# Block products for the first gated step, block sums on GpSimd, and an order that favours open PSUM banks

## The chip, the cores and the metric

The kernel runs on one core of one Trainium2 chip. The metric is the device time of one execution in microseconds; the kernel before takes 1395.11 us (median of three runs, 1395.05 to 1396.01). The profile of one execution has a span of 1394.1 us from its first to its last instruction; the runs lie about 1 us above it.

## What is computed

The input is `x`, 64 samples of 256 nodes with 128 features, float32, and one 256 x 256 adjacency matrix `adj` that all samples share. Four graph layers follow one another, each in the frame `x = layernorm(x + layer(x))`: two attention layers, a gated layer of five steps, and a Chebyshev layer of order three. For this change the gated layer (layer 2) matters most:

```python
def step(h, _):
    m_in = jnp.einsum('nm,bmd->bnd', in_matrix, h)     # adj @ h, the "left product"
    m_out = jnp.einsum('nm,bmd->bnd', out_matrix, h)   # the same matrix here
    av = jnp.concatenate([m_in, m_out], axis=-1)
    u3 = h @ u3_w.T + u3_b
    z = jax.nn.sigmoid(av @ w3_w.T + w3_b + u3)
    r = jax.nn.sigmoid(av @ w4_w.T + w4_b + u3)
    hv = jnp.tanh(av @ w5_w.T + w5_b + (r * h @ u5_w.T + u5_b))
    h = (1.0 - z) * h + z * hv
```

Layer 3 needs one more left product, `adj @ x`.

## The kernel before

**Units and lanes.** The 64 samples are worked off in 32 units of two samples. Ten lanes of SBUF buffers hold ten units at a time; `spawn` lists all four layers of a unit as tasks, and when a unit is done its lane takes the next one. So up to ten units, each in another layer or step, share the engines.

**The order.** No engine order is written by hand. Every instruction is a `Task` with an engine, an assumed duration, what it reads and writes, and the PSUM banks that it uses. `Plan.run` plays these tasks through in advance with the assumed durations and latencies: whenever an engine is free it takes, of the tasks that are ready, the one with the smallest key, `first(t)`: the place of the unit in the queue times 43 us plus the task's due time in the unit. A task that opens a PSUM bank (`t.takes`) is ready only if one of the eight banks is free. The order so found is the order in which each engine's instructions stand; on the chip each engine works its own list from the front, and semaphores hold back an instruction whose inputs are not there.

**The left product, plain form.** `left` (L812 to L818) makes `adj @ h` for one sample by two matmuls of 128x256; a unit of two samples needs four. ScalarE then copies the bank into `m` (L886). A float32 matmul appears in the trace as two records, so the four are eight records of line L816.

**The left product, fast form.** `left_fast` (L820) treats the 256 x 256 matrix as 2 x 2 blocks of 128 and the unit's two samples as two columns of blocks, and does the 2 x 2 by 2 x 2 block product by seven block products rather than eight (Winograd's form of Strassen's method):

- Four block sums of the operand `h`, in three VectorE instructions, L826 (two blocks at once, 128x256), L828 and L829 (128x128 each), into the tile `four`, which lies on the lane's buffer `r`; the trace calls that buffer `e`. The sums of the matrix blocks are made once, at the start, on GpSimd (L476 to L480), in two layouts, `adjTf` for steps 1 to 4 and `adjf` for layer 3.
- Seven matmuls of 128x128 (L833) into two banks `x` and `y`; three read blocks of `h`, four read block sums.
- A ScalarE copy of one product (L845) and four VectorE additions (L860, L863, L865, L866) that merge the products into `m`.

`FAST = (1, 2, 3, 4, 5)` says where the fast form is used: steps 1 to 4 of layer 2, and 5 is layer 3's left product; step 0 uses the plain form. Units 0 and 1 and the last unit use the plain form in some steps (`far`).

**The rest of a step.** L890 makes five products of 128x512 into two banks: `gT[3]` with `h`, three of gate weights with `m`, and `u5T` with the reset state. ScalarE applies tanh three times (L901, L909, L918), VectorE combines (L904, L916, L920, L922), transposes in blocks (L930), and two hops of DMA through DRAM (L933, L936) bring the new state back in the layout that the next left product reads. Where a list of tasks is given as `after`, the product waits for them as well; `lefts[1:2]` in L895 lets the product with `h` follow the second left product of its own step.

**GpSimd** before makes the small steps of the layer norms (L584 to L595) and little else.

Of the kernel before, what the change touches and what calls it, by code (L numbers as in the profile page):

```python
# [16 lines left out]
STEPS = 5  # L17
LANES = 10
LEAD = 10
BANKS = 8  # L20
BL = 32
FAST = (1, 2, 3, 4, 5)
NORM = (0, 1, 2, 3)
SCALES = True
SMALL = ("ve", "cu", "d", "elu", "shift")
# [6 lines left out]
PERIOD = 43e3  # L32
TAIL = 0.3
LATE = 6
# [3 lines left out]
DIRECT_ROWS = 3  # L38
XDIRECT = 10
START = 35e3  # L40
R2 = 1
R3 = 1.5

# [23 lines left out]
class Plan:  # L67
# [17 lines left out]
    def add(self, eng, ns, fn, reads=(), writes=(), after=(), wait=0, group=None, dma=False):  # L85
        t = Task(eng, ns, fn, self.unit, wait, dma or eng == "sp")
        for c in reads:
            t.deps.update(c.writers)
            c.readers.append(t)
        for c in writes:  # L90
            if c.bank and not c.writers:
                t.takes.append(c)
            if group is None or c.group is not group:
                c.waits = {w for o in (c, *c.over) for w in (*o.writers, *o.readers)} - {t}
                c.writers, c.readers, c.group = [], [], group
            t.deps.update(c.waits)
            if c.bank and c.writers:

                t.deps.add(c.writers[0])
            c.writers.append(t)  # L100
        t.deps.update(after)
        t.deps.discard(t)
        for c in {id(c): c for c in (*reads, *writes) if c.bank}.values():
            c.users += 1
            t.banks.append(c)
        t.step = self.step = self.step + 1
        t.layer = self.layer
        t.rank = self.rank
        self.tasks.append(t)
        return t  # L110
# [90 lines left out]
def kernel(  # L201
# [28 lines left out]
    nc = tc.nc  # L230
# [3 lines left out]
    NU = B // UB  # L234
    T = UB * N
    G = UB * NC
    PE, DVE, ACT, POOL = "pe", "dve", "act", "pool"
# [12 lines left out]
    plan = Plan([psum.tile([P, 512], F32, tag=f"ps{k}", name=f"ps{k}") for k in range(BANKS)])  # L250
    add = plan.add
# [142 lines left out]
    def product(ps, at, n, lhs, lhs_ap, rhs, rhs_ap):  # L394
        add(PE, mm_ns(n), lambda: nc.tensor.matmul(ps.ap[:, at : at + n], lhs_ap(), rhs_ap(), start=True, stop=True,
                                                   skip_group_check=True), (lhs, rhs), (ps,))
# [50 lines left out]
    gT = transposed("gT", [(gs[0], gs[0].ap), (gs[1], gs[1].ap), (gs[2], gs[2].ap), (u3, u3.ap)])  # L447
# [35 lines left out]
    adjTf = fast_blocks("adjTf", adjTp)  # L483
    adjf = fast_blocks("adjf", adjT) if 0 in FAST or STEPS in FAST else None
# [21 lines left out]
    X = {}  # L506

    def gd(ap):
        return ap.rearrange("p (g d) -> p g d", g=G)
# [307 lines left out]
                ps.ap[:, b * N : (b + 1) * N], lhs(b, mc), mat.ap[:, mc, :],  # L817
                start=(mc == 0), stop=(mc == NC - 1)), (src, mat), (ps,))  # L818

    def left_fast(src, blk, mat, s, p1, m):  # L820


        four = gd(s.ap)
        ss = object()

        add(DVE, 360, lambda: nc.vector.tensor_sub(  # L826
            four[:, 0:2], blk(slice(2, 3)).to_broadcast([P, 2, D]), blk(slice(0, 4, 3))), (src,), (s,), group=ss)
        add(DVE, 220, lambda: nc.vector.tensor_sub(four[:, 2:3], four[:, 1:2], blk(slice(0, 1))), (src, s), (s,), group=ss)  # L828
        add(DVE, 220, lambda: nc.vector.tensor_add(four[:, 3:4], four[:, 2:3], blk(slice(1, 2))), (src, s), (s,), group=ss)  # L829
        x, y = bank(), bank()  # L830

        def one(ps, at, lhs, k, c, cells, after=()):
            add(PE, mm_ns(P) + 4, lambda: nc.tensor.matmul(  # L833
                ps.ap[:, at * P : (at + 1) * P], lhs(), mat.ap[:, k, c * P : (c + 1) * P], start=True, stop=True,
                skip_group_check=True), (*cells, mat), (ps,), after, group=four)

        def a(g):
            return lambda: blk(slice(g, g + 1))[:, 0]

        def sm(k):  # L840
            return lambda: four[:, k]


        one(x, 0, a(0), 0, 0, (src,))
        add(ACT, 280, lambda: nc.scalar.copy(p1.ap[:, 0:P], x.ap[:, 0:P]), (x,), (p1,))  # L845
        one(x, 1, a(1), 1, 0, (src,))
        one(y, 3, a(3), 3, 1, (src,), s.writers[-1:])
        one(y, 1, sm(0), 3, 0, (s,))
        one(y, 0, sm(1), 2, 0, (s,))
        one(x, 2, sm(2), 2, 1, (s,))  # L850
        one(y, 2, sm(3), 1, 1, (s,))
        mv = gd(m.ap)

        ms = object()

        def pv(ps):
            return gd(ps.ap)


        add(DVE, 400, lambda: nc.vector.tensor_tensor(  # L860
            mv[:, 0:4:3], pv(x)[:, 1:3], p1.ap[:, 0:P].rearrange("p (o n) -> p o n", o=1).to_broadcast([P, 2, P]), op=ALU.add),
            (x, p1), (m,))
        add(DVE, 400, lambda: nc.vector.tensor_tensor(  # L863
            mv[:, 1:3], pv(y)[:, 0:2], mv[:, 3:4].to_broadcast([P, 2, P]), op=ALU.add), (y, m), (m,))
        add(DVE, 240, lambda: nc.vector.tensor_add(mv[:, 3:4], pv(y)[:, 0:1], mv[:, 2:3]), (y, m), (m,))  # L865
        add(DVE, 400, lambda: nc.vector.tensor_add(mv[:, 1:3], pv(y)[:, 2:4], mv[:, 1:3]), (y, m), (m,))  # L866

    def layer2(u, L):
        h, ht = turned(u, L, -1), X[u]
        for step in range(STEPS):  # L870
            m, at = L["m"], len(plan.tasks)
            fast = step in FAST and far(u, step - 1)
            ps_m = None if fast else bank()
            if fast and not step:
                left_fast(ht, lambda g: ht.ap.rearrange("p b c d -> p (b c) d")[:, g], adjf, L["r"], L["z"], m)
            elif fast:
                left_fast(ht, lambda g: gd(ht.ap)[:, g], adjTf, L["r"], L["z"], m)
            for b in range(0 if fast else UB):
                if ht is X[u]:
                    left(ps_m, ht, b)  # L880
# [8 lines left out]
            def product(ps, w, c, rhs, start, stop, after=()):  # L889
                add(PE, mm_ns(T), lambda: nc.tensor.matmul(ps.ap, w(), rhs.ap, start=start, stop=stop,  # L890
                                                           skip_group_check=True), (c, rhs), (ps,), after)


            lefts = [t for t in plan.tasks[at:] if t.eng == PE]
            product(ps_g, lambda: gT.ap[:, 3], gT, h, True, False, lefts[1:2])  # L895
            product(ps_g, lambda: gT.ap[:, 1], gT, m, False, True)
            r, z, v = L["r"], L["z"], L["v"]

# [14 lines left out]
            if not step:  # L913
                add(ACT, 600, lambda h=h, new=new, part=part: nc.scalar.mul(new.ap, h.ap, part), (h,), (new,))
                h = new
# [54 lines left out]
    def layer3(u, L):  # L970
        xT = turned(u, L, STEPS)
        aT, s = L["m"], L["z"]
        if STEPS in FAST and far(u, STEPS):
            left_fast(X[u], lambda g: X[u].ap.rearrange("p b c d -> p (b c) d")[:, g], adjf, L["r"], L["z"], aT)
            tail = [t for t in plan.tasks[-4:-3]]
        else:
            ps_a = bank()
            for b in range(UB):
                left(ps_a, X[u], b)
            add(ACT, 500, lambda: nc.scalar.copy(aT.ap, ps_a.ap), (ps_a,), (aT,))  # L980
            tail = list(ps_a.writers)

        ps = [bank() for _ in range(NC)]

        def view(c):
            return ps[c].ap.rearrange("p (k b d) -> p k b d", k=2, b=UB)

        for k, src in enumerate((xT, aT)):
            for c in range(NC):
                for b in range(UB):  # L990
                    add(PE, mm_ns(N), lambda k=k, src=src, c=c, b=b: nc.tensor.matmul(  # L991
                        view(c)[:, :, b, :], bn(src.ap)[:, b, c * P : (c + 1) * P], w3.ap[:, k],
                        start=(k == 0 and b == 0), stop=(k == 1), skip_group_check=True), (src, w3), (ps[c],), tail)
        for c in range(NC):
            add(ACT, 300, lambda c=c: nc.scalar.copy(s.ap[:, c * N : (c + 1) * N], ps[c].ap[:, N : 2 * N]), (ps[c],), (s,), group=ps)
        for c in range(NC):
            for mc in range(NC):
                add(PE, mm_ns(N), lambda c=c, mc=mc: nc.tensor.matmul(  # L998
                    ps[c].ap[:, 0:N], a2T.ap[:, mc, c * P : (c + 1) * P], s.ap[:, mc * N : (mc + 1) * N],
                    start=False, stop=(mc == NC - 1), skip_group_check=True), (a2T, s), (ps[c],))  # L1000
        pairs = [(ps[c], lambda c=c: view(c)[:, 0]) for c in range(NC)]
        if u >= NU - 2:
            layernorm_last(u, pairs)
            return
        layernorm(u, L, pairs, swap=True)
        add("sp", 450, lambda: nc.sync.dma_start(out_u[u], X[u].ap), (X[u],), ())
# [10 lines left out]
    def first(t):  # L1017
        if t.rank is not None:
            return t.rank * PERIOD
        if t.unit < 0:  # L1020
            return t.due - 1e6
        return (t.unit if t.unit < NU - LANES else NU - 1 - LATE - (NU - 1 - t.unit) * TAIL) * PERIOD + t.due

    with tc.manual_schedule():
        for t in plan.run(spawn, range(NU), first):
# [31 lines left out]
```

The softmax here doesn't subtract the row's maximum and nothing guards it: scores larger than these inputs give would overflow.

## Time and profile before

| what | value |
|---|---|
| time, median of 3 | 1395.11 us |
| span in the profile | 1394.1 us |
| L890, matmul 128x512, all forms, chain share | 49% |
| L833, matmul 128x128, chain share | 17% |
| L816, matmul 128x256, chain share | 5% |
| L886, ScalarE copy of a plain left product | 39 times, 585 ns each |
| L860, L863, L865, L866, the merge of a fast one | 152 times each; 417, 418, 281, 413 ns |
| L845, ScalarE copy in the fast form | 152 times, 267 ns |

The chain share says how much of the span lies on the chain of work that ended last, by line. Mean durations are those of one instruction on its engine. The busy time of a matmul record is modelled, and records overlap, so a matmul's cost on TensorE is read from the distance between the starts of successive records and not from its mean duration.

### The profile page before, as it was taken

Reading aid. Unit: us, or ns where it says so; the run is one execution under the profiler, and the core shown is the slowest. Engines: PE = TensorE matmul, PEld = TensorE weight load, DVE = VectorE, ACT = ScalarE, POOL = GpSimd, SP = SyncE. Lnnn points to the kernel's source line nnn. Section 1 sums busy time; section 2 is a strip of 40 time slices with the busy share of each in tenths; the row PEclk is TensorE's granted clock in tenths of the full one; section 3 lists DMA queues with packets and bytes.
Section 4 is the critical chain, followed back from the end, with each engine's and each line's share of the span. In section 5 each row is a group of like instructions: output and inputs, shape, how many; then the busy total and the mean of one; then the engine's idle time right before and its main releaser. Section 6 shows DMA issues by size and latency. Waiting matters only on the chain.

```text
span 1394.1 us, 21842 instructions
## 1 busy us (share of the span) xinstructions
PE 1385.5 (99%) x6537; PEld 963.8 (69%) x6537; DVE 1191.1 (85%) x2849; ACT 911.2 (65%) x2094; POOL 257.9 (18%) x488
## 2 busy tenths in 40 slices
PE   9999999999999999999999999999999999999998
PEld 8776576776666766676676667676666666667776
DVE  6788898999988888888898899889888888999763
ACT  6887636556765767666676778787755555565454
POOL 3111020112112112122121122132111110112212
PEclk9999999999999999999999999999999999999999
DMA  4134554455455454554455555554463543544521
GB/s 126 32 62 99 114 120 86 117 108 131 109 114 112 98 130 95 122 127 102 108 108 111 128 110 110 118 114 103 108 129 94 119 105 86 115 114 106 129 52 47
DMA packets 530068, 147.03 MB, mean 105 GB/s; under 512 B 456480, under 2 KB 495136, under 8 KB 529952
## 3 DMA queue, kind: packets, MB, share of 16 engines
q1 hardware_dynamic: 529152, 145.13, 46.6%
q8 instruction: 52, 0.85, 0.3%
q14 instruction: 64, 0.52, 0.2%
q10 hardware_dynamic: 800, 0.52, 0.1%
HBM read 81.10 MB, written 64.46 MB: 104 GB/s over the span
## 4 chain that ended last, share of the span: by engine, by line
PE 98%; ACT 1%; DVE 1%; DMA 0%; issue 0%; SPq 0%; POOL 0%; POOLq 0%; DVEq 0%; ACTq 0%
PE ps L890 49%; PE ps L833 17%; PE ps L991 8%; PE ps L816 5%; PE ps L738 4%; PE ps L998 4%; PE ps L775 4%; PE ps L787 2%; PE ps L733 2%; PE ps L662 2%; ACT p L711 0%; DMA u<-rowu 0%; PE ps L348 0%; PE ps L955 0%; PE ps L528 0%; PE ps L571 0%
## 5 line engine op out<-in xcount | busy, mean ns | idle before, releaser
L890 PE MATMUL ps<-m,gT 128*128 128x512 f32 x960 | 464.1, 593 | 0.0
L890 PEld LDWEIGHTS ps<-m,gT 128*128 128x128 f32 x960 | 170.8, 190 | 124.9 <-issue 107.8
L909 ACT ACTIVATE e<-ps,bias 128x512 f32<-128x512 f32 x160 | 109.7, 687 | 159.0 <-PE ps L890 156.5
L901 ACT ACTIVATE e<-ps,bias 128x512 f32<-128x512 f32 x160 | 109.9, 687 | 98.9 <-PE ps L890 97.0
L833 PEld LDWEIGHTS ps<-adjTf,ht 128*128 128x128 f32 x726 | 117.6, 191 | 74.3 <-issue 60.1
L584 POOL TENSOR_SCALAR ve<-st 128x4 f32<-128x4 f32 x110 | 36.3, 330 | 690.5 <-DVE st L582 662.3
L890 PE MATMUL ps<-e,u5T 128*128 128x512 f32 x320 | 162.4, 592 | 0.0
L587 POOL TENSOR_TENSOR rstd<-ve,nhalf 128x4 f32<-128x4 f32 x126 | 142.0, 1127 | 66.5 <-DVE ve L584 59.5
L833 PEld LDWEIGHTS ps<-adjTf,e 128*128 128x128 f32 x968 | 127.4, 192 | 19.2 <-issue 17.7
L833 PE MATMUL ps<-adjTf,e 128*128 128x128 f32 x968 | 139.6, 275 | 0.0
L918 ACT ACTIVATE p<-ps,bias 128x512 f32<-128x512 f32 x160 | 110.2, 689 | 40.5 <-PE ps L890 38.4
L833 PE MATMUL ps<-adjTf,ht 128*128 128x128 f32 x726 | 123.7, 275 | 0.3 <-DVE m L860 0.3
L920 DVE SCALAR_TENSOR_TENSOR p<-e,p 128x512 f32<-128x512 f32 x160 | 109.4, 685 | 16.5 <-ACT p L918 16.0
L890 PEld LDWEIGHTS ps<-e,u5T 128*128 128x128 f32 x320 | 59.3, 190 | 61.4 <-issue 51.6
L890 PE MATMUL ps<-xT,gT 128*128 128x512 f32 x192 | 97.5, 594 | 0.4 <-ACT xT L530 0.4
L860 DVE TENSOR_TENSOR m<-ps,e 128x256 f32<-128x256 f32 x152 | 63.0, 417 | 25.1 <-PE ps L833 21.2
L764 ACT ACTIVATE e<-m,esd 128x256 f32<-128x256 f32 x116 | 82.2, 766 | 0.0
L904 DVE SCALAR_TENSOR_TENSOR e<-e,xT 128x512 f32<-128x512 f32 x96 | 65.7, 684 | 15.5 <-ACT e L901 13.5
L863 DVE TENSOR_TENSOR m<-ps,m 128x256 f32<-128x256 f32 x152 | 63.3, 418 | 16.0 <-PE ps L833 14.1
L541 DVE STREAM_TRANSPOSE p<-x 128x512 f32<-128x512 f32 x61 | 67.3, 1104 | 11.1 <-ACT x L606 11.0
L738 PEld LDWEIGHTS ps<-ht,p 128*128 128x128 f32 x512 | 65.9, 190 | 12.9 <-issue 12.0
L738 PE MATMUL ps<-ht,p 128*128 128x130 f32 x512 | 68.5, 274 | 0.0
(191 smaller groups left out, 2784.0 us busy)
## 6 DMA issues: line engine op xcount, KB each, us to landing
hb<-p SPq DMA_DIRECT2D x182, 256.0 KB, 2.3
ht<-hb SPq DMA_DIRECT2D x484, 64.0 KB, 2.6
xT<-hb SPq DMA_DIRECT2D x244, 64.0 KB, 2.5
m<-row SPq DMA_DIRECT2D x58, 256.0 KB, 3.8
hb<-p SPq DMA_DIRECT2D x124, 64.0 KB, 1.8
ht<-hb SPq DMA_DIRECT2D x31, 256.0 KB, 3.0
out_dram<-x SPq DMA_DIRECT2D x30, 256.0 KB, 2.4
m<-in_x_dram SPq DMA_DIRECT2D x88, 64.0 KB, 2.3
```

Source lines behind the costliest of these rows:

```text
L541: add(DVE, 1050, lambda: nc.vector.transpose(v.ap.rearrange("p (a g i) -> p g a i", g=G, i=BL), X[u].ap.rearrange("p b c (j a) -> p (b c) ...
L587: add(POOL, 1050, lambda: nc.gpsimd.tensor_tensor(rstd.ap, ve.ap, nhalf.ap, op=ALU.pow), (ve, nhalf), (rstd,))
L738: add(PE, mm_ns(D + 2), lambda b=b, ic=ic, kc=kc, yv=yv: nc.tensor.matmul(yv()[:, ic, :], p.ap[:, b * NC + kc, ic * P : (ic + 1) * P], h.a ...
L764: add(ACT, 600, lambda g=g, b=b: nc.scalar.activation(e.ap[:, g, :].rearrange("p (c n) -> p c n", c=NC), ev()[:, b], AF.Prelu, bias=esd.ap ...
L816: add(PE, mm_ns(N), lambda b=b, mc=mc: nc.tensor.matmul(ps.ap[:, b * N : (b + 1) * N], lhs(b, mc), mat.ap[:, mc, :], start=(mc == 0), stop ...
L833: add(PE, mm_ns(P) + 4, lambda: nc.tensor.matmul(ps.ap[:, at * P : (at + 1) * P], lhs(), mat.ap[:, k, c * P : (c + 1) * P], start=True, st ...
L890: add(PE, mm_ns(T), lambda: nc.tensor.matmul(ps.ap, w(), rhs.ap, start=start, stop=stop, skip_group_check=True), (c, rhs), (ps,), after)
L901: add(ACT, 600, lambda ps_g=ps_g, up=up: nc.scalar.activation(r.ap, ps_g.ap, AF.Tanh, bias=bias2.ap[:, 1:2], scale=0.5 / up), (ps_g, bias2 ...
L909: add(ACT, 600, lambda ps_g=ps_g, up=up: nc.scalar.activation(z.ap, ps_g.ap, AF.Tanh, bias=bias2.ap[:, 0:1], scale=0.5 / up), (ps_g, bias2 ...
L918: add(ACT, 600, lambda ps_v=ps_v, up=up: nc.scalar.activation(v.ap, ps_v.ap, AF.Tanh, bias=bias2.ap[:, 2:3], scale=1 / up), (ps_v, bias2), ...
L920: add(DVE, 600, lambda: nc.vector.scalar_tensor_tensor(v.ap, z.ap, 1.0, v.ap, op0=ALU.add, op1=ALU.mult), (v, z), (v,))
L991: add(PE, mm_ns(N), lambda k=k, src=src, c=c, b=b: nc.tensor.matmul(view(c)[:, :, b, :], bn(src.ap)[:, b, c * P : (c + 1) * P], w3.ap[:, k ...
```

## The change

It does four things. Step 0 joins `FAST`, so the gated layer's first left product is made by seven block products too. `BY_POOL` moves the three block-sum instructions from VectorE to GpSimd, in all six places, with durations of their own for the planner. In fast steps, the product with `h` now follows the third merging addition and not the second block product, so that its bank is opened later. And `HASTE` takes 20 us off the planner's key for a TensorE, ScalarE or VectorE task that works on a PSUM bank that is already open, so that banks are emptied and closed sooner. (`ht=ht` in the lambdas only binds the tile at that time.)

```diff
-FAST = (1, 2, 3, 4, 5)
+FAST = (0, 1, 2, 3, 4, 5)
+BY_POOL = (0, 1, 2, 3, 4, 5)
...
+HASTE = {"pe": 20e3, "act": 20e3, "dve": 20e3}
...
-    def left_fast(src, blk, mat, s, p1, m):
+    def block_sums(src, blk, s, by_pool):
         four = gd(s.ap)
         ss = object()
-        add(DVE, 360, lambda: nc.vector.tensor_sub(
+        by, eng = (POOL, nc.gpsimd) if by_pool else (DVE, nc.vector)
+        wide, narrow = (830, 480) if by_pool else (360, 220)
+        add(by, wide, lambda: eng.tensor_sub(
             four[:, 0:2], blk(slice(2, 3)).to_broadcast([P, 2, D]), blk(slice(0, 4, 3))), (src,), (s,), group=ss)
-        add(DVE, 220, lambda: nc.vector.tensor_sub(four[:, 2:3], four[:, 1:2], blk(slice(0, 1))), (src, s), (s,), group=ss)
-        add(DVE, 220, lambda: nc.vector.tensor_add(four[:, 3:4], four[:, 2:3], blk(slice(1, 2))), (src, s), (s,), group=ss)
+        add(by, narrow, lambda: eng.tensor_sub(four[:, 2:3], four[:, 1:2], blk(slice(0, 1))), (src, s), (s,), group=ss)
+        add(by, narrow, lambda: eng.tensor_add(four[:, 3:4], four[:, 2:3], blk(slice(1, 2))), (src, s), (s,), group=ss)
+        return four
+
+    def left_fast(src, blk, mat, s, p1, m, by_pool):
+        four = block_sums(src, blk, s, by_pool)
...
             lefts = [t for t in plan.tasks[at:] if t.eng == PE]
-            product(ps_g, lambda: gT.ap[:, 3], gT, h, True, False, lefts[1:2])
+            merge = plan.tasks[at:][-4:]
+            product(ps_g, lambda: gT.ap[:, 3], gT, h, True, False, merge[2:3] if fast else lefts[1:2])
...
-        return (t.unit if t.unit < NU - LANES else NU - 1 - LATE - (NU - 1 - t.unit) * TAIL) * PERIOD + t.due
+        soon = HASTE.get(t.eng, 0) if t.banks and not t.takes else 0
+        return (t.unit if t.unit < NU - LANES else NU - 1 - LATE - (NU - 1 - t.unit) * TAIL) * PERIOD + t.due - soon
```

More of the change, by code (lines that the diff above doesn't have):

```diff
@@ L874, in layer2 @@
             if fast and not step:
-                left_fast(ht, lambda g: ht.ap.rearrange("p b c d -> p (b c) d")[:, g], adjf, L["r"], L["z"], m)
+                left_fast(ht, lambda g, ht=ht: ht.ap.rearrange("p b c d -> p (b c) d")[:, g], adjf, L["r"], L["z"], m, step in BY_POOL)
             elif fast:
-                left_fast(ht, lambda g: gd(ht.ap)[:, g], adjTf, L["r"], L["z"], m)
+                left_fast(ht, lambda g, ht=ht: gd(ht.ap)[:, g], adjTf, L["r"], L["z"], m, step in BY_POOL)
             for b in range(0 if fast else UB):
@@ L973, in layer3 @@
         if STEPS in FAST and far(u, STEPS):
-            left_fast(X[u], lambda g: X[u].ap.rearrange("p b c d -> p (b c) d")[:, g], adjf, L["r"], L["z"], aT)
+            left_fast(X[u], lambda g: X[u].ap.rearrange("p b c d -> p (b c) d")[:, g], adjf, L["r"], L["z"], aT, STEPS in BY_POOL)
             tail = [t for t in plan.tasks[-4:-3]]
```

## The prediction

> **What bounds the kernel now.** I read the page's busy times first, then its chain of waits, then TensorE alone in order of time, because busy time by itself misleads there.
>
> ```profile
> PE 1385.5 (99%) x6537; PEld 963.8 (69%) x6537; DVE 1191.1 (85%) x2849; ACT 911.2 (65%) x2094; POOL 257.9 (18%) x488
> ...
> PE 98%; ACT 1%; DVE 1%; DMA 0%; issue 0%; SPq 0%; POOL 0%; POOLq 0%; DVEq 0%; ACTq 0%
> ```
>
> The second line: the chain that ended last is TensorE from one end to the other, with 2% for anything else. Whether TensorE is also packed shows in the starts of successive records (start us, us, engine, line, count):
>
> ```profile
> 603.07 0.83 PE L833 MATMUL ps<-adjTf,e 128*128 128x128 f32 x6
> 603.74 1.89 PE L816 MATMUL ps<-adjT,x 128*128 128x256 f32 x8
> 605.47 1.89 PE L991 MATMUL ps<-w,m 128*128 128x256 f32 x8
> ```
>
> Six records of 128x128 take 603.74 - 603.07 = 0.67 us, 0.112 each; eight of 128x256 take 1.73 us, 0.216 each. L890's 128x512 read the same way gives 0.430. Over the whole timeline, distances beyond these (where over 0.04 us) sum to 5.6 us: 1.8 among the warm-up products of the first 5 us, 3.1 from there to 75 us, 0.7 in all the rest. So TensorE hardly ever waits. A change gains what it takes off TensorE's list and loses what it makes TensorE wait; work moved between other engines gains nothing by itself.
>
> **What the Trainium skill says.** "Perfetto Trace Analysis", Identifying the Most-Contended Engine: matmul occupancy is a poor measure, since matmuls are pipelined. The trace agrees: a 128x512 record is shown 593 ns long, and the next starts after 430. "TensorE: Matmul & The Clock Gate", Wait — 56ns, not 53.3ns?: N / 2.4 GHz + 2.5 ns between starts, 55.6 at N = 128 and 215.7 at N = 512. The records here take twice that, so a small product pays hardly more per column than a large one; that makes seven small ones cheaper than four of twice the width. Two more places are used below.
>
> **The change part by part.**
>
> *Step 0's products, on the path.* The changed program's order has 40 plain products of 128x256 instead of 160, and 1274 block products instead of 1064: 30 of 32 units change. Each drops 8 records x 0.216 = 1.73 us and takes 14 x 0.112 = 1.56, 0.165 us less. Times 30: **5.0 us off TensorE**, 0.36%.
>
> *Step 0 off the path.* ScalarE loses 30 copies of 585 ns (L886) and gets 30 of 267 (L845): 9.5 us less of 911, nothing on the path. VectorE gets 30 x (417 + 418 + 281 + 413 ns) = 46 us of merges. Block sums below.
>
> *Block sums to GpSimd.* VectorE rows that go (operation, tiles, count | busy us, mean ns | idle before):
>
> ```profile
> L826 DVE TENSOR_TENSOR e<-ht 128x256 f32<-128x256 f32 x121 | 49.6, 411 | 0.1
> ...
> L829 DVE TENSOR_TENSOR e<-e,ht 128x128 f32<-128x128 f32 x121 | 34.4, 284 | 1.0
> L828 DVE TENSOR_TENSOR e<-e,ht 128x128 f32<-128x128 f32 x121 | 34.1, 282 | 0.4
> ```
>
> With the 31 that read `x` (12.4 + 8.8 + 8.7) that is 148 us. VectorE was not the bound, so its relief of 148 - 46 = 102 us counts only through rarer late merges: at most part of the 0.7 us above. GpSimd gets 3 x 182 = 546 instructions. Their price is read from the start of the kernel, where GpSimd makes sums of the same kind:
>
> ```profile
> 10.65 0.45 POOL L476 TENSOR_TENSOR adjTf<-adjTf 128x128 f32<-128x128 f32 x1
> ...
> 13.80 0.18 POOL L451 TENSOR_TENSOR bias<-biases 128x1 f32<-128x1 f32 x1
> ```
>
> 0.45 us at 128 columns and 0.18 at one: 2.13 ns per column. "GPSIMD Engine Reference", 3.1, has 2.6 cycles per element at 1.2 GHz, 2.17 ns, the same. The two-block sum then takes 0.45 + 128 x 0.00213 = 0.72 us, and the three 1.62, against 0.98 (411 + 284 + 282 ns) on VectorE: the sums come at least 0.65 us later.
>
> *Contention.* "SBUF — State Buffer", Who interferes with whom: a VectorE instruction with two SBUF inputs and a GpSimd one that reads SBUF shut each other out for a whole instruction. Both directions show in the trace. GpSimd behind VectorE: L584 takes 195 ns where no VectorE instruction overlaps it and 381 in the mean where one does; this is its row in all:
>
> ```profile
> L584 POOL TENSOR_SCALAR ve<-st 128x4 f32<-128x4 f32 x110 | 36.3, 330 | 690.5 <-DVE st L582 662.3
> ```
>
> VectorE behind GpSimd: the same two-input addition once with GpSimd idle, and twice while GpSimd is adding:
>
> ```profile
> 7.41 0.29 DVE L420 TENSOR_TENSOR wself<-wself,ident 128x128 f32<-128x128 f32 x1
> ...
> 8.85 0.93 DVE L434 TENSOR_TENSOR mask<-adjT,ident 128x128 f32<-128x128 f32 x2
> ```
>
> 0.29 against 0.46 each, 0.18 more. For the sums I take 0.15 us per GpSimd instruction, 2.1 us for three. The low end is 1.62; the high end, where each waits for one 685 ns instruction (L904's mean), is 1.62 + 2.06 = 3.7. GpSimd in all: 258 + 182 x 2.1 = 640 us, 46%, far from a bound. VectorE: 768 two-input instructions (640 of L904, L916, L920, L922 and 128 of L768, L807, L808, L961), estimated 30% of them delayed by 0.2 us, add 46 us: 1191 - 102 + 46 = 1135, 81%, under what it carries now.
>
> *The wait that this adds.* Four of seven products read sums. If a sum is late, TensorE stands, and with it every lane's products behind it, since TensorE works its list in order. How much room is there? Following each lane's `four` tile from the end of L829 to the first L833 record that reads it, the sums are ready 3.8 us ahead in the median, 2.1 at the lower quarter, 1.0 at the lower twentieth and 0.3 at the least. The new planner durations (830 + 480 + 480 = 1790 ns in place of 800) place the products about 1 us later, which is what the sums lose at my value (2.1 - 0.98 = 1.1). So the room should stay as it is, less some scatter. I take **0.6 us** of new stalls; zero at the low end, and at the high end a quarter of the 182 sums late by 0.3 us, 14 us.
>
> *The product with `h` after the third merge.* It no longer covers the merge on TensorE (0.86 us), so other lanes must. In the changed order the first product with `m` still stands 2.6 us or more of TensorE work after the last block product (2.2 before, at these distances per record), while L860, L863, L865 and L866 need 1.53 us. Nothing, hidden by other lanes' products; a step may last longer, but ten lanes overlap.
>
> *The open-bank preference* reorders everything and removes no work: TensorE's list falls from 2672 runs of like instructions to 2296, since products into one bank now follow each other. Records into one bank are as dense as those into two (L816 and L991 above), so nothing in the middle. At the end it helps: before, the last two units' final norms fall together and ScalarE runs four L631 instructions in one row from 1389.31 to 1390.96; after, the second-last finisher's products stand 18 above the end, so two remain. One ScalarE instruction of 0.4 us: **0.4 us less**.
>
> Sum: 1395.1 - 5.0 + 0.6 - 0.4 = **1390.3 us**.
>
> **The rivals.**
>
> *Late sums (slower).* The sums take 3.7 us, every late one stops TensorE. For it: locks shown above, GpSimd's norms of 1.1 us (L587) in the same queue. Against it: the room, and GpSimd's 54% of idle time. 1395.1 - 5.4 + 14 = 1404.
>
> *The gain is given back by the new order (no change).* The preference starves some lanes' bank openings, or the first 75 us get stalls like the 3.1 us there now. For it: in the opening few lanes have work, and the whole list changes. Against it: nothing in the middle depends on one order. Stalls of 4 us more: 1394.
>
> *The order also fills the opening.* Most of the 3.1 us of stalls before 75 us vanish, VectorE's relief takes part of the 0.7: 1390.3 - 2.3 = 1388.0.
>
> **How the numbers follow.** Work saved and order neutral 67%, at 1390.3 with about 1.5 us to either side; opening filled too 10%, at 1388; given back 13%, 1392.5 to 1396; late sums 10%, 1397 and beyond. The bound of 0.2% is 2.8 us, below 1392.3. Faster: the first two and a little of the third, 78%; same: most of the third and a little of the fourth, 13%; slower 9%. The range goes from 1387.6, the filled opening, to 1394.0, and leaves out the late sums and part of the third case.
>
> **What would show it.** Right: line 816's successor with 80 records and not 320, the block products 2548 records at 0.112 us spacing, TensorE's chain share at 98%, distances beyond the spacing still summing to 5 or 6 us, GpSimd busy 560 to 700 us, VectorE 1090 to 1150. Wrong: TensorE's weight loads or products waiting for GpSimd's `e` in the list of waits, in sum over 2 us (late sums); gaps in the first 75 us above 5 us (opening); VectorE above 1190 us, which would mean locks far more costly than 0.2 us; or a last product more than 6.5 us ahead of the end.

## The result, and the profile after

The changed kernel takes 1390.75 us (median of 4 runs, 1390.18 to 1391.60) against 1395.56 us for the kernel before on the same chips (4 runs, 1395.05 to 1396.54): ratio 0.9964, 95% interval 0.9950 to 0.9978. It was forecast at 1390.3. In the changed file the lines below the first edits stand a little lower: L816 is now L818, L833 is L841, L890 is L898, the block sums are L830, L832 and L833, the merge is L868, L871, L873 and L874.

The page of the changed kernel, busy time by engine and the chain of waits by engine and by line:

```profile
PE 1380.8 (99%) x6717; PEld 965.0 (69%) x6717; DVE 1149.7 (83%) x2513; ACT 903.6 (65%) x2094; POOL 623.4 (45%) x1034
...
PE 97%; DVE 2%; ACT 1%; DMA 0%; issue 0%; POOL 0%; SPq 0%; POOLq 0%; DVEq 0%; ACTq 0%
PE ps L898 49%; PE ps L841 20%; PE ps L1000 8%; PE ps L1007 4%; PE ps L777 4%; PE ps L740 4%; PE ps L789 2%; PE ps L735 2%; PE ps L664 2%; PE ps L818 1%; ACT p L713 0%; DVE e L695 0%; DMA u<-rowu 0%; PE ps L350 0%; PE ps L964 0%; DVE nm L705 0%
```

TensorE is still the chain. It has 180 more records and 4.7 us less busy time: block products went from 17% to 20% of the chain and the plain left product from 5% to 1%. GpSimd went from 258 to 623 us. The spacing of records, in TensorE's order of time, is what it was:

```profile
602.56 0.83 PE L841 MATMUL ps<-adjf,e 128*128 128x128 f32 x6
603.23 0.39 PE L841 MATMUL ps<-adjTf,ht 128*128 128x128 f32 x2
603.45 0.83 PE L841 MATMUL ps<-adjTf,e 128*128 128x128 f32 x6
604.12 1.88 PE L898 MATMUL ps<-m,gT 128*128 128x512 f32 x4
605.84 1.46 PE L777 MATMUL ps<-p,x 128*128 128x256 f32 x6
```

Six records from 602.56 to 603.23 and six from 603.45 to 604.12 take 0.67 us each time, 0.112 per record, and four of 128x512 take 1.72.

Since TensorE carries the time, I split each profile's span into three terms, in the same way for all runs below. **Stalls** are the distances between successive starts beyond 0.113 us (up to 133 columns), 0.216 (256) or 0.430 (512), where they exceed 0.04 us. **List** is the end of the last TensorE record less the stalls (the first record starts at 1.3 us). **End** is what follows the last record.

| kernel | span | list | stalls (before 75 us, 75 to 1300, later) | end | ratio of times to before, 95% interval |
|---|---|---|---|---|---|
| before | 1394.1 | 1382.4 | 5.6 (4.9, 0.7, 0.0) | 6.0 | 1 |
| changed | 1389.4 | 1377.8 | 6.0 (5.2, 0.5, 0.3) | 5.6 | 0.9964 [0.9950, 0.9978] |
| step 0 alone | 1399.2 | 1377.6 | 15.5 (4.6, 10.9, 0.0) | 6.1 | 1.0036 [1.0023, 1.0048] |
| without step 0 | 1393.9 | 1382.6 | 5.7 (5.1, 0.3, 0.3) | 5.6 | 0.9998 [0.9990, 1.0006] |
| without the preference | 1394.5 | 1377.8 | 10.9 (4.9, 4.6, 1.3) | 5.9 | 1.0004 [0.9996, 1.0012] |
| sums on VectorE | 1396.1 | 1377.8 | 12.4 (5.2, 7.0, 0.3) | 5.9 | 1.0013 [1.0006, 1.0019] |
| half the units | 1394.0 | 1380.2 | 8.2 (4.5, 2.9, 0.8) | 5.6 | 1.0003 [0.9995, 1.0011] |
| wide sum twice | 1412.4 | 1377.9 | 28.9 (5.4, 23.2, 0.3) | 5.6 | 1.0131 [1.0117, 1.0145] |
| early product with h | 1391.9 | 1377.8 | 8.5 (4.2, 4.0, 0.3) | 5.6 | 0.9988 [0.9980, 0.9996] |
| step 0 alone, true durations and due times | 1436.1 | 1377.9 | 52.1 (4.9, 46.0, 1.3) | 6.0 | 1.0291 [1.0277, 1.0305] |
| step 0 alone, true durations | 1424.8 | 1377.6 | 41.1 (4.7, 33.5, 3.0) | 6.1 | 1.0216 [1.0202, 1.0230] |
| changed, true durations | 1396.6 | 1377.8 | 12.8 (5.5, 7.0, 0.3) | 6.0 | 1.0014 [1.0007, 1.0020] |
| preference 10 us | 1392.7 | 1377.7 | 9.4 (5.7, 2.8, 1.0) | 5.6 | 0.9987 [0.9980, 0.9993] |
| preference 40 us | 1391.3 | 1377.6 | 8.2 (6.5, 1.1, 0.5) | 5.6 | 0.9983 [0.9976, 0.9989] |

The list has three values in the table, and which one applies depends on the number of fast step-0 products alone: 1382.5 with none, 1380.2 with 15 units, 1377.7 with 30. What a kernel gains or loses beyond that is stalls, and up to 0.5 us at the end. (Each row is one profile; the time of a run lies 1 to 2.4 us above its span, and compares with before only on its own chip. The spans of the changed kernel's four runs go from 1388.3 to 1389.7 us, so a microsecond between two rows says little.)

One caution holds for all the experiments but one. A kernel in which a part is undone or altered is planned anew, and its engines get another order throughout; its stalls come from that part and from the new order together. Only "wide sum twice" keeps the changed kernel's order.

### The profile page after: what moved, and what is told of

It reads as the page before. It is cut to its first block, busy times and chain, and to the rows that moved or that the text cites. A ratio compares the mean times of both kernels' runs of the same rounds, so it can differ in the third digit from the quotient of the medians.

```text
span 1389.4 us, 22566 instructions
## 1 busy us (share of the span) xinstructions
PE 1380.8 (99%) x6717; PEld 965.0 (69%) x6717; DVE 1149.7 (83%) x2513; ACT 903.6 (65%) x2094; POOL 623.4 (45%) x1034
## 4 chain that ended last, share of the span: by engine, by line
PE 97%; DVE 2%; ACT 1%; DMA 0%; issue 0%; POOL 0%; SPq 0%; POOLq 0%; DVEq 0%; ACTq 0%
PE ps L898 49%; PE ps L841 20%; PE ps L1000 8%; PE ps L1007 4%; PE ps L777 4%; PE ps L740 4%; PE ps L789 2%; PE ps L735 2%; PE ps L664 2%; PE ps L818 1%; ACT p L713 0%; DVE e L695 0%; DMA u<-rowu 0%; PE ps L350 0%; PE ps L964 0%; DVE nm L705 0%
## 5 line engine op out<-in xcount | busy, mean ns | idle before, releaser
L898 PE MATMUL ps<-m,gT 128*128 128x512 f32 x960 | 473.7, 592 | 0.0
L898 PEld LDWEIGHTS ps<-m,gT 128*128 128x128 f32 x960 | 171.1, 191 | 132.4 <-issue 115.7
L898 PE MATMUL ps<-e,u5T 128*128 128x512 f32 x320 | 163.1, 592 | 0.0
L830 POOL TENSOR_TENSOR e<-ht 128x256 f32<-128x256 f32 x121 | 98.6, 815 | 142.5 <-DMA ht<-hb 100.0
L929 DVE SCALAR_TENSOR_TENSOR p<-e,p 128x512 f32<-128x512 f32 x160 | 116.3, 727 | 41.7 <-ACT p L927 41.0
L841 PE MATMUL ps<-adjTf,e 128*128 128x128 f32 x968 | 148.2, 275 | 0.1
L841 PEld LDWEIGHTS ps<-adjTf,e 128*128 128x128 f32 x968 | 131.5, 192 | 20.1 <-issue 18.0
L841 PEld LDWEIGHTS ps<-adjTf,ht 128*128 128x128 f32 x726 | 109.1, 191 | 46.7 <-issue 43.0
L841 PE MATMUL ps<-adjTf,ht 128*128 128x128 f32 x726 | 120.4, 274 | 0.0
L898 PEld LDWEIGHTS ps<-e,u5T 128*128 128x128 f32 x320 | 58.9, 190 | 63.8 <-issue 52.1
L898 PE MATMUL ps<-xT,gT 128*128 128x512 f32 x192 | 98.2, 593 | 0.0
L871 DVE TENSOR_TENSOR m<-ps,m 128x256 f32<-128x256 f32 x182 | 75.0, 413 | 22.5 <-PE ps L841 20.9
L830 POOL TENSOR_TENSOR e<-x 128x256 f32<-128x256 f32 x61 | 48.5, 796 | 99.0 <-ACT x L608 87.1
L868 DVE TENSOR_TENSOR m<-ps,e 128x256 f32<-128x256 f32 x182 | 74.6, 414 | 19.5 <-PE ps L841 12.1
L853 ACT COPY e<-ps 128x128 f32<-128x128 f32 x182 | 47.9, 265 | 49.6 <-PE ps L841 47.3
L832 POOL TENSOR_TENSOR e<-e,ht 128x128 f32<-128x128 f32 x121 | 76.9, 635 | 6.9
```

Source lines behind the costliest of these rows:

```text
L830: add(by, wide, lambda: eng.tensor_sub(four[:, 0:2], blk(slice(2, 3)).to_broadcast([P, 2, D]), blk(slice(0, 4, 3))), (src,), (s,), group=ss)
L832: add(by, narrow, lambda: eng.tensor_sub(four[:, 2:3], four[:, 1:2], blk(slice(0, 1))), (src, s), (s,), group=ss)
L841: add(PE, mm_ns(P) + 4, lambda: nc.tensor.matmul(ps.ap[:, at * P : (at + 1) * P], lhs(), mat.ap[:, k, c * P : (c + 1) * P], start=True, st ...
L871: add(DVE, 400, lambda: nc.vector.tensor_tensor(mv[:, 1:3], pv(y)[:, 0:2], mv[:, 3:4].to_broadcast([P, 2, P]), op=ALU.add), (y, m), (m,))
L929: add(DVE, 600, lambda: nc.vector.scalar_tensor_tensor(v.ap, z.ap, 1.0, v.ap, op0=ALU.add, op1=ALU.mult), (v, z), (v,))
```

## The experiments

### Which part of the change brings the gain

My theory was the one of the prediction: the gain is TensorE's shorter list, and other engines' relief brings nothing. The rival was that the relief or the order brings it. Four kernels, each the changed one with parts undone:

```diff
# step 0 alone
-BY_POOL = (0, 1, 2, 3, 4, 5)
+BY_POOL = ()
-HASTE = {"pe": 20e3, "act": 20e3, "dve": 20e3}
+HASTE = {}
-            product(ps_g, lambda: gT.ap[:, 3], gT, h, True, False, merge[2:3] if fast else lefts[1:2])
+            product(ps_g, lambda: gT.ap[:, 3], gT, h, True, False, lefts[1:2])
# without step 0
-FAST = (0, 1, 2, 3, 4, 5)
+FAST = (1, 2, 3, 4, 5)
# without the preference: HASTE = {} alone
# sums on VectorE: BY_POOL = () alone
```

> Step 0 in the fast form and nothing else: block sums on VectorE, no open-bank preference, the product with h after the second block product as before. If the gain is TensorE's shorter list (theory of work): 30 units x 0.165 us less, 5.0 us under the kernel before, give or take 1. If the gain comes from VectorE's relief or from the order (rival, theory of relief): none of it is here and VectorE carries 30 x (0.98 + 1.53) = 75 us more, some 1266 us or 91% busy, so late merges make TensorE wait: 0 to 8 us slower than before.

> The whole change without its first part: step 0 keeps the plain left product; sums on GpSimd, the later product with h and the open-bank preference stay. Work: TensorE's list is that of before, so within 1.5 us of before. Relief: most of the 4.8 us remain, 3 us or more under before.

> The whole change without the open-bank preference. Work: the same list in another order, within 1 us of the changed kernel, and at the end the two last units' norms may fall together again (0.4 us more). Relief by the order: the gain is mostly gone, 3 to 5 us above the changed kernel.

> The whole change with the block sums left on VectorE, now 182 times 0.98 us. VectorE then carries about 1150 - 60 of lock waits + 178 = 1265 us, 91%. Work: TensorE still has room, within 1.5 us of the changed kernel. Relief of VectorE: merges come late, 3 us or more above the changed kernel.

Step 0 alone took 1401.05 us, 0.36% slower than before. Without step 0 the time was 1396.03 against 1396.12 for before: the other parts by themselves bring nothing. Without the preference 1396.72 and with the sums on VectorE 1397.76: with either of them undone, the whole gain is gone. So neither theory stands as I put it. The list is shorter by 4.5 to 5.0 us wherever all 30 units have the fast step 0, as mine says, but it becomes time only where TensorE can work the shorter list with few waits. Of these kernels, only the one with all the parts does.

In the kernel with step 0 alone such a wait can be followed. First the busy times of a stretch of 300 us, before and then with step 0 alone (columns: stretch, length, busy us of TensorE, its weight loads, VectorE, ScalarE, GpSimd, each with its count; clock, DMA share, GB/s):

```profile
900.00:1200.00 300.00, 300.00 (x1354) 200.96 (x1353) 261.97 (x608) 190.71 (x427) 48.47 (x95) 1.00 0.48 107
```

```profile
900.00:1200.00 300.00, 297.89 (x1395) 200.06 (x1393) 274.10 (x667) 187.40 (x427) 49.78 (x90) 1.00 0.49 108
```

VectorE goes from 87% to 91%, and TensorE now has gaps. The longest of them, in order of time with step 0 alone:

```profile
925.45 0.23 DVE L745 TENSOR_TENSOR esd<-ps,rstd 128x4 f32<-128x4 f32 x2 [0.46 <-ACT x L608]
...
925.65 1.16 ACT L608 ACTIVATE x<-ps,ones,rstd 128x128 f32<-128x128 f32 x3 [0.23 <-DVE esd L745]
...
926.16 0.71 PE L841 MATMUL ps<-adjTf,ht 128*128 128x128 f32 x4 [1.41 <-ACT x L608]
926.40 0.42 DVE L874 TENSOR_TENSOR m<-ps,m 128x256 f32<-128x256 f32 x1
...
926.87 0.30 PEld L898 LDWEIGHTS ps<-m,gT 128*128 128x128 f32 x2 [0.18 <-DVE m L874]
```

TensorE is idle for 1.41 us until a norm of ScalarE (L608, `x<-ps`) has read out a PSUM bank. That norm had waited for VectorE (L745), and L745 for an earlier L608, with VectorE idle for 0.46 us before it. So VectorE's load is not the whole of it: lists that are worked in order wait for each other. After that the product with `m` still has to wait for another lane's merge: L874 ends at 926.82, the weight load starts at 926.87. The same wait, of TensorE's weight loads for the last merging addition, in the lists of waits of the changed kernel, of the one without the preference and of the one with the sums on VectorE (us in total, times, longest). A weight load that waits a little need not hold a product back: the changed kernel has 3.9 us of these waits and 0.5 us of stalls in its whole middle.

```profile
PEld ps L898 <- DVE m L874: 3.9, 15, 0.5
```

```profile
PEld ps L898 <- DVE m L874: 6.4, 19, 1.0
```

```profile
PEld ps L898 <- DVE m L874: 10.0, 24, 1.5
```

What the preference does is not to bring the sums sooner. Followed as in the prediction, the sums are ready 6.5 us ahead of their first product in the median without it, and 2.9 with it. But the merge comes sooner: from the start of a unit's last block product record to the end of its last merging addition it takes 2.9 us in the median and 5.4 at the upper twentieth without the preference, 2.5 and 3.9 with it. That this is the whole of the 4.9 us of stalls is not shown.

With the sums on VectorE the merges are not slower as a rule: 2.4 us in the median and 3.8 at the upper twentieth, though the longest takes 8.0 and not 5.7. What differs is the order. Counted as in the prediction, at the distances per record, TensorE's list there has as little as 1.3 us of work between a unit's last block product and its first product with `m`; the changed kernel's has 2.6 or more. So these stalls show what a plan with the sums on VectorE costs, and not simply a VectorE that is too slow.

### Half a dose, and the product with h

```diff
# half the units
-            fast = step in FAST and far(u, step - 1)
+            fast = step in FAST and far(u, step - 1) and (step > 0 or u % 2 == 0)
# early product with h
-            product(ps_g, lambda: gT.ap[:, 3], gT, h, True, False, merge[2:3] if fast else lefts[1:2])
+            product(ps_g, lambda: gT.ap[:, 3], gT, h, True, False, lefts[1:2])
```

> The changed kernel, with step 0 in the fast form for every second unit alone (15 units instead of 30). Theory of the sum (time = TensorE's list + its stalls + the end): half of the 4.8 us of list come back, stalls stay near 6 us, so 2 to 3 us above the changed kernel and as much under the kernel before. Rival, a threshold (the new order works only as a whole): at either end, within 1 us of the one or the other.

> The changed kernel with one part undone: the product with h follows the second block product again, not the third merging addition. My prediction priced this part at nothing: within 1 us of the changed kernel. Rival: holding the bank open over the merge starves other lanes of banks, or the merge is no longer what TensorE waits for: 2 us or more to one side.

Half the units: 1396.40 us, no gain against before (1395.93). By the number this is what the rival had named, within 1 us of one end. The list does lie halfway, at 1380.2; what failed is my expectation of unchanged stalls, which grew from 6.0 to 8.2 us. So the list follows the dose, and the time does not.

The early product with `h`: 1394.27, about two thirds of the gain lost. Its profile has 3.5 us more of stalls in the middle (4.0 for 0.5) and 1.0 less before 75 us. I had priced that part at nothing. The merge is not what TensorE waits longer for: its weight loads wait 3.3 us for L874, where the changed kernel has 3.9. The waits of weight loads and products for GpSimd's sums grew, from 1.2 to 7.1 us. Whether that comes from the bank that is held open or from the new order stays open.

### How much room the sums have

```diff
-        add(by, wide, lambda: eng.tensor_sub(
-            four[:, 0:2], blk(slice(2, 3)).to_broadcast([P, 2, D]), blk(slice(0, 4, 3))), (src,), (s,), group=ss)
+        add(by, wide, lambda: [eng.tensor_sub(
+            four[:, 0:2], blk(slice(2, 3)).to_broadcast([P, 2, D]), blk(slice(0, 4, 3))) for _ in range(2)], (src,), (s,), group=ss)
```

> The changed kernel, with the wide block sum (128x256, GpSimd) issued twice, 182 instructions of 0.73 us more that the planner does not know of; every engine's order is otherwise the same. The sums come 0.8 us later. Room: 9 of 182 sums are less than 0.8 us ahead of their first product, with 5 us missing in sum if no stall gave room to the next. Sums with room (my step in the prediction): 1 to 5 us above the changed kernel. Rival, GpSimd's queue or the port lock is already at its edge: 8 us or more.

It took 1414.46 us, 23 us of stalls more, far beyond what I had allowed and well past the rival's 8 us. TensorE, ScalarE and VectorE have the same order as in the changed kernel, and the list of waits names the cause:

```profile
PEld ps L841 <- POOL e L832: 20.7, 22, 3.5
PE ps L841 <- POOL e L832: 11.5, 11, 3.3
```

In the changed kernel TensorE's waits for GpSimd's sums come to 1.2 us in all. One instruction of 0.73 us more makes TensorE wait over 3 us for single sums. Here is the longest such wait, first GpSimd and then TensorE, in order of time:

```profile
145.25 1.55 POOL L830 TENSOR_TENSOR e<-x 128x256 f32<-128x256 f32 x2 [1.76 <-ACT x L608]
146.88 0.78 POOL L832 TENSOR_TENSOR e<-e,x 128x128 f32<-128x128 f32 x1
147.74 0.78 POOL L833 TENSOR_TENSOR e<-e,x 128x128 f32<-128x128 f32 x1
148.48 2.30 POOL L830 TENSOR_TENSOR e<-ht 128x256 f32<-128x256 f32 x2
150.86 0.78 POOL L832 TENSOR_TENSOR e<-e,ht 128x128 f32<-128x128 f32 x1
```

```profile
151.70 0.49 PE L841 MATMUL ps<-adjTf,e 128*128 128x128 f32 x2 [3.26 <-POOL e L832]
```

The sums of one unit (those that read `ht`) stand behind those of another (`x`) in GpSimd's list, so the delay of the first is added to their own; and two wide sums take 2.30 us here, 1.55 there. Both the queue and the slower single instruction count, and how the 23 us divide between them was not measured. Room counted lane by lane sees neither.

Counted as in the prediction, from the end of the third sum (L833) to the first product that reads the tile, the sums are ready 1.7 us ahead in the median and 0.2 at the lower quarter, where the changed kernel has 2.9 and 1.8; in 37 of 182 cases the product starts before the third sum has ended. It can, because it does not wait for that one: the waits above name L832, the second sum. Counted from the second, the room is 2.6 us in the median, 1.0 at the lower quarter and 0.05 at the lower twentieth, and 3.9, 2.6 and 1.4 in the changed kernel.

### Is the order stale, or is it a lucky draw?

The planner assumes 600 ns for VectorE instructions that take 685. Could the stalls of step 0 alone come from that? In one kernel the planner was told measured durations everywhere, in two only where it plays the tasks through, so that the due times stayed:

```diff
+        t.real = {600: 690, 1050: 1105, 360: 411, 220: 283, 400: 417, 240: 281, 330: 423, 520: 610, 120: 160, 1150: 1216}.get(ns, ns) if eng == "dve" and self.unit >= 0 else ns
...
-                free[e] = t.off = now + t.ns
+                free[e] = t.off = now + t.real
```

> Step 0 alone in the fast form, sums on VectorE, no preference, as in the run of step 0 alone that came out 5 us above before; but the planner is told VectorE's measured durations (690 in place of 600 ns, 1105 for 1050, 411 for 360, 283 for 220, and so on). If the 10 us of stalls there come from an order that counts on a faster VectorE (theory of the stale plan): most of them go, 1391 to 1394. If they come from VectorE's load as such (88 to 91% busy, theory of capacity): they stay, 1398 or more.

> Step 0 alone in the fast form once more (sums on VectorE, no preference), with VectorE's measured durations used only where the planner plays the tasks through; the due times that rank them stay as they were, while in the run that came out at 1437.6 they had grown too. TensorE's list is 1377.6 us in any case. Stale plan (the order counts on a faster VectorE): stalls fall from 15.5 to 6 to 9 us, 1391 to 1395. Capacity (a VectorE at 88 to 91% makes TensorE wait in any order): 13 us of stalls or more, 1398 or above; then the 1437.6 came from the ranking on top.

> The changed kernel, with VectorE's measured durations where the planner plays the tasks through, due times as they were. Its stalls in the middle are 0.5 us already, so there is next to nothing to gain: within 1.5 us of 1390.8 if the low stalls come from relief and room (theory of room). If the changed kernel's order is one good draw among many (theory of scatter): 2 to 6 us above it, as with half the units (stalls 8.2) or the early product with h (8.5).

1437.64, 1426.57 and 1397.89 us: every one is worse than with the wrong durations, by 37 and 26 us for step 0 alone and by 7 for the changed kernel. The theory of the stale plan falls. The first two lie in the range that I had set for capacity, 1398 or more, but a full VectorE doesn't explain the third: its VectorE is 83% busy, as in the changed kernel, and its stalls are 12.8 us and not 6.0. No part of the change is missing there. I had set 1.5 us for a kernel whose low stalls come from room, and 2 to 6 for one good order among many; 7 speaks for the second. Why truer durations give a worse order stays open.

Last, the size of the preference:

```diff
-HASTE = {"pe": 20e3, "act": 20e3, "dve": 20e3}
+HASTE = {"pe": 10e3, "act": 10e3, "dve": 10e3}     # and 40e3
```

> The changed kernel with the open-bank preference halved, 10 us in place of 20. Without it the stalls are 10.9 us, with 20 us they are 6.0. Room: a smooth dependence, stalls 6 to 9 us, 1390.5 to 1394. Scatter: anywhere from 1390 to 1399, with no order between 0, 10, 20 and 40 us.

> The changed kernel with the open-bank preference doubled, 40 us in place of 20. Room: banks close at least as early, stalls 5 to 7 us, 1389.5 to 1392. Scatter: anywhere from 1390 to 1399.

At 0, 10, 20 and 40 us the stalls between 75 and 1300 us are 4.6, 2.8, 0.5 and 1.1, and in all 10.9, 9.4, 6.0 and 8.2. With 40 us I had expected 5 to 7 in all and at most 1392 us; it took 1393.72. The four values look like a dependence, but each is one order, and kernels that keep the preference at 20 us lie as far apart (6.0 changed, 8.2 with half the units, 12.8 with true durations). So scatter of the orders is not ruled out, and 20 us may in part be a good draw. At 1393.89 and 1393.72 us both sizes beat the kernel before. Their ratios are 0.9987 and 0.9983 against the 0.9964 of 20 us; the interval of the second still touches that of 20 us. No kernel tried is faster than the changed one.

## Why the prediction was right, and where its reasons were not

The span of the profile fell by 4.7 us. The terms below add up to that: 4.6 us less of list, 0.5 less at the end (6.05 to 5.58 before rounding), 0.4 more of stalls.

**TensorE's list, 5.0 us less:** 1382.4 to 1377.8, 4.6; against the kernel without step 0, 4.8. This is the term that carries the result, and half a dose took half of it off the list.

**The end, 0.4 us less:** 6.0 to 5.6, and in the way that was foreseen. The changed kernel's last instructions, in order of time:

```profile
1385.57 0.46 ACT L633 ACTIVATE x<-ps,ve,rstd 128x128 f32<-128x128 f32 x1 [1.93 <-DVE ve L631]
...
1386.23 0.46 ACT L633 ACTIVATE x<-ps,ve,rstd 128x128 f32<-128x128 f32 x1 [0.21 <-DVE ve L631]
```

Two such instructions and not four in a row. The preference alone doesn't bring that about: the kernel with the sums on VectorE and the changed one with true durations have it too, and their ends are 5.9 and 6.0.

**New stalls, 0.6 us:** 5.6 to 6.0. The size is right, but the three steps behind it do not carry it. I took the relief of VectorE as worth at most part of the 0.7 us that the kernel before loses in the middle. That was measured on a kernel without 46 us of new merges; the changed kernel with the sums on VectorE has 6.4 us more of stalls (12.4 against 6.0). I took the open-bank preference for neutral in the middle, since "nothing in the middle depends on one order": without it, 4.9 us more. And the later product with `h` was "Nothing, hidden by other lanes' products": 2.5 us more with that part undone. How much of each is the part and how much the new order is not separated, as 6.8 us more with no part undone show. But the sentence on the order is wrong either way: the stalls in the middle went from 0.5 to 7.0 us there, by the order alone. I had priced each part against the kernel before, and not against the kernel with the first part in place, and had no number for what another order costs. That the stalls came out within 0.2 us of the forecast is therefore luck, as far as these steps go.

**Block sums on GpSimd:** 2.1 us forecast for three, 1.99 measured (147.1 + 106.6 + 108.7 us in 182 times); 640 us of GpSimd forecast, 623 measured. The wide sum on `ht`, in the groups of GpSimd:

```profile
L830 POOL TENSOR_TENSOR e<-ht 128x256 f32<-128x256 f32 x121 | 98.6, 815 | 142.5 <-DMA ht<-hb 100.0 <-PE ps L898 34.0 <-PE ps L841 7.5
L832 POOL TENSOR_TENSOR e<-e,ht 128x128 f32<-128x128 f32 x121 | 76.9, 635 | 6.9
```

Where no VectorE instruction overlaps, they take 0.726 and 0.457 us, for 0.72 and 0.45 forecast.

**Room:** I wrote that it should stay as it is. Counted the same way, it went from 3.8 to 2.9 us in the median, from 2.1 to 1.8 at the lower quarter and from 1.0 to 0.8 at the lower twentieth, enough for the sums as they are: TensorE waits 1.2 us for them, under the 2 us that I had named as a sign of late sums. The count itself was too strict by one sum, as the experiment with the wide sum shows. The high end of that step was mis-sized: 14 us for sums 1.6 us later than my value, where 0.73 us of GpSimd more cost 23. The rival of late sums was nearer than the chance I gave it.

**VectorE:** 1135 us forecast, 1150 measured. More of its instructions meet GpSimd than I took, and each loses less: 56% of L913, L925, L929 and L931 overlap a GpSimd instruction, where I took 30% as delayed, but in the mean an overlap costs 0.05 to 0.08 us and not 0.2, 26 us in all. The rest is in the counting. The durations summed fell by 73 us, from 1377 to 1303, close to what 102 us of relief less 26 us of delay give. But instructions one right behind the other overlap in the trace, by 186 us in sum before and 154 after, and busy time counts an overlap once; so busy time fell by 41 us only.

## What to carry to other kernels

On an engine that is packed from end to end, split the time into its list, its stalls and the end, and look at the three apart. The cut of the list came out in every kernel here that had the fast step 0; whether it became time was decided by the stalls, which another order moved by as much as the cut was worth. Price each part of a change against the kernel that has the other parts in it. And where a planner makes the order, undoing a part also draws a new order: before its cost is put down to the part, change something that should not matter and see how far that moves the time. Last, count room at the queue of the engine that delivers, not from one producer to one consumer: a small delay there is passed on to what stands behind.

## What the runs showed of the hardware

- GpSimd's block sums hold up VectorE's instructions with two SBUF inputs, and not the merging additions. In the changed kernel L913, L925, L929 and L931 (two SBUF inputs, 128x512) take 0.68 us apart from GpSimd and 0.73 to 0.76 in the mean where one of its instructions overlaps, with single ones up to 1.25. The merging additions, with one input in PSUM, take 0.41 us either way (L868: 0.414 apart, 0.413 overlapped). The Trainium skill ("SBUF — State Buffer", Who interferes with whom) says that a VectorE instruction with two SBUF inputs contends with a GpSimd one that reads SBUF, and one with at most one SBUF input does not; the means agree.
- Most overlaps cost VectorE nothing: the median of the overlapped ones is 0.683 to 0.693 us, and the delay sits in a minority of them (0.93 to 0.99 us at the upper tenth). In the kernel before, where GpSimd makes mostly the small steps of the norms, the same instructions (L904, L916, L920, L922 there) overlap it 142 times in 640 and take 0.68 to 0.69 us in the mean, as they do apart. In the other direction GpSimd's L584 there takes 195 ns apart from VectorE and 381 in the mean with it.
- GpSimd's 128x256 addition of float32 takes 0.726 us undisturbed and that of 128x128 0.457, in the spans that the trace shows: 2.1 ns for a further column.
